# Gate product, inverse denominators and layer norm moved within a step of a scan-attention pipeline; routing and expert order and layout changed

## The chip, the cores and the metric

The kernel runs on one core of one Trainium2 chip. The metric is the time of one execution on the device in microseconds (us). Five engines work side by side, each through its own instructions in order: PE (TensorE; its weight loads are shown as PEld), DVE (VectorE), ACT (ScalarE), POOL (GpSimd) and SP (SyncE, which here only starts DMAs). They wait for each other on semaphores.

## The reference, cut to what matters

```python
# layer 0, x: (16, 128, 64, 64); 4096 positions a picture
u = gn(x) as tokens;  xs, z = split(u @ W_in)          # 2 x 256 channels
xc = silu(causal_conv4(xs) + conv_b)
dt, Bm, Cm = split(xc @ W_xproj)                       # 8, 16, 16
delta = softplus(dt @ W_dt + b_dt)
h = exp(delta * A) * h + delta * xc * Bm               # scan over positions, 16 states n
y = sum_n(h * Cm) + xc * D_param
x = x + (y * silu(z)) @ W_out
# layer 1, t: tokens of x
k, v = silu(ln(t) @ W_kv)                              # 8 heads
s = q . k;  m = cummax(s);  e = exp(s - m)
t = t + mean_over_heads(cumsum(e * v) / cumsum(e))
p = softmax over tokens of ln(t) @ gate_w.T            # 64 experts take their top 8 tokens
out_e = gelu(pooled_e @ weight1) @ weight2             # pooled: the 8 tokens weighted by p
t = t + scatter_add(out_e * p at the chosen tokens)
```

## The kernel before

**First stage: 137 steps.** A picture is 8 blocks of 512 positions, so there are 128 blocks. Step k (`for k in range(NK + LAG + 1)`, L712) scans block k. In the same step block k - 1 is finished (its y is turned, gated with z, multiplied by W_out), block k + 1 is prepared (convolution, projection, delta), and attention is done on block m = k - 9, whose second half is done one step later under the name `mp_`; layer norm of block m + 1 is done under the name `mn`. The last nine steps have attention only.

A step is a loop over the 16 states n (L898). In it, DVE multiplies bx = delta * xc * B (`product`, L355, 128 x 1024), then scans two halves of channels (`scan`, L361, 128 x 512 each); POOL multiplies h by C into the tile da (L375), and for odd n up to 7 starts a DMA that adds da of n - 1 onto da of n (`add_pair`). PE sums the 16 products over n by transposing matmuls into y_ps (`add_y`, `sums_of_y`, L892). ACT makes exp(delta * A) ahead of time: `decays(k, n, 2)` makes the next two tiles da. The rows B and C come broadcast from DRAM to bct (`load_bc`, by SP, three n ahead).

All engines are held to the order in which the program is written (`InOrder`, L23). So `beside(n)` (L736) is a list of what goes beside state n, written ahead of the scan, and `between(n)` (L724) is what DVE does between the two scans of n. A tile's buffers are handed out when the program is built. Matmul results go through three PSUM banks (`bank`, L224), which all the products of attention, convolution and projection share: a PE instruction that takes a bank waits for the instruction that last read it.

The functions of this change: `gate(k, a)` (L417, DVE) multiplies half a of the turned y, in PSUM as yb_ps, by z; it frees the bank of yb_ps. `conv` (L286) is the causal convolution as four matmuls per half into xs_ps, `conv_silu` (L295) its silu into xc on ACT, and `delta` (L324) two matmuls of 8 rows (dt_ps) and a softplus. `ln_center` (L456) makes cen_ps on PE, `ln_square` (L461) its square on ACT, `ln_var` (L466) var_ps on PE, `ln_scale` (L471) rstd on ACT (a Ln and an Exp), and `ln_apply` (L477) xn = cen * rstd on DVE at n = 14. `score_log`, `rest` and `split` (L553 to L578) cut two vectors in three bf16 parts each, `store_parts` (L580) writes them to DRAM, and `spread_parts` (L585) has SP read them back in 16 small DMAs into lh and rh. `weights` (L606) makes from lh and rh the exponents w_ps and on ACT the weights wm; `attend` (L623) multiplies them with v into ao_ps and sums the carry of a chunk, `carry_on` (L644) copies that carry on ACT, and `attend_before` (L648) adds the earlier chunks' part with e. `inverse` (L560) makes e, four Exps of 128 x 128. `gn_end` (L242) is group norm of the next picture, in parts that alternate between DVE, PE and ACT; it happens in the last but one step of a picture.

A table load on ACT (ACT_TABLE_LOAD) comes where the kind of function changes: into Exp/Ln (`load_exp`, L218) and back to Silu or Softplus.

**Second stage: routing** (L943 to L1134). 64 iterations, each over 512 tokens of two pictures, with work of 14 more behind them: PE turns the tokens (x_ps) and makes logits (l_ps); DVE takes mean and variance (`stats`), ACT makes rs, DVE nm and the scaled logits ls; PE turns ls into s_ps and ACT adds a bias into lg (`turn_logits`, L1028); ACT normalises the tokens in eight instructions into xn (`normed`, L1040). `choose` (L1055) takes the top 8 of each expert every eight iterations, `turn_chosen` and `pool_chosen` sum the chosen tokens, `turn_pooled` (L1101) turns the sums of a pair of pictures.

**Third stage: experts** (L1139 to L1180). 16 groups of four experts: SP loads w1 and w2, PE makes the hidden layer hps, ACT Gelu, PE turns it in four transposes, DVE copies, and PE multiplies by w2. **Fourth stage** (L1183): the experts' outputs are added to the tokens, unchanged here.

Of the kernel before, what the change touches and what calls it, by code (L numbers as in the profile page):

```python
# [8 lines left out]
F32 = mybir.dt.float32  # L9
# [6 lines left out]
P = 128  # L16
# [23 lines left out]
def conv_attn_hybrid(ctx: ExitStack, tc: tile.TileContext, x, w_in, conv_w, conv_b, w_xproj, w_dt, b_dt,  # L40
# [40 lines left out]
    with ExitStack() as st:  # L81
# [139 lines left out]
        def softplus(out_, in_, bias):  # L221
            ACT.activation(out_, in_, AF.Softplus, bias=bias)

        def bank(name):  # L224
            return ps.tile([P, L], F32, tag="ps", name=name)
# [98 lines left out]
        def delta(k):  # L324
            w = blocks[k]
            d = w["delta"] = mp.tile([P, NH2, L], F32, tag="delta", name="delta")
            for a in range(NH2):
                pt = bank("dt_ps")
                PE.matmul(pt, wdt[:, bass.ts(a, P)], w["dbl"][:R, :], start=True, stop=True)
                softplus(d[:, a, :], pt, bdt[:, a : a + 1])  # L330

        def delta_x(k):
            w = blocks[k]
# [378 lines left out]
        for k in range(NK + LAG + 1):  # L712
# [10 lines left out]

            def between(n):  # L724

                if m is not None:
                    if n == 4:
                        score_less(m)
                    if n == 6:
                        score_sum(m)  # L730
                if ends is not None and n == 5:
                    gn_end(ends, 2)
                if n == 15 and nxt is not None:
                    delta_x(nxt)

            def beside(n):  # L736
# [51 lines left out]
                    if ends is not None:  # L788
                        gn_end(ends, 1)
                if n == 5:  # L790
                    if prev is not None:
                        gate(prev, 1)
                    if mp_ is not None:
                        attend(mp_, 2)
                    if m is not None:
                        score_exp(m)
                    decays(k, n, 2)
                    if mp_ is not None:
                        carry_on(mp_, 2)
                        attend_before(mp_, 2)  # L800
                if n == 6:
                    if mp_ is not None:
                        weights(mp_, 3)
                    if prev is not None:
                        out_proj(prev)
                    if mp_ is not None:
                        attend(mp_, 3)
                    decays(k, n, 2)
                    if prev is not None:
                        put_back(prev)  # L810
                    if mp_ is not None:
                        carry_on(mp_, 3)
                    if ends is not None:
                        gn_end(ends, 3)
                if n == 7:
                    if m is not None:
                        score_log(m)
                        rest(m, 1)
                        split(m, 1)
                    if nxt is not None:  # L820
                        conv(nxt, 1, range(KC // 2))
                    decays(k, n, 2)
                    if m is not None:
                        rest(m, 2)
                        split(m, 2)
                        store_parts(m)
                        inverse(m)
                    if nxt is not None:
                        conv(nxt, 1, range(KC // 2, KC))
                        conv_silu(nxt)  # L830
                if n == 8:
                    if cur is not None:
                        sums_of_y(n)
                    if mp_ is not None:
                        attend_before(mp_, 3)
                        add_x(mp_, 1)
                        finish(mp_, 1)
                    if m is not None:
                        turn_weights(m)
                        value(m, 0, 0)  # L840
                    if nxt is not None:
                        xproj(nxt)
                        store_bc(nxt)
                    if m is not None:
                        value(m, 0, 1)
                    if ends is not None:
                        gn_end(ends, 4)
                if n == 9:
                    if mn is not None:
                        ln_center(mn)  # L850
                        ln_square(mn)
                    if cur is not None:
                        gate_silu(cur)
                    if k + 2 < NK:
                        load_block(k + 2, ACT)
                    if m is not None:
                        value(m, 1, 0), value(m, 1, 1)
                if n == 10:
                    if mn is not None:
                        ln_var(mn)  # L860
                    if nxt is not None:
                        delta(nxt)
                    load_exp()
                    if mn is not None:
                        ln_scale(mn)
                if n == 11:
                    if m is not None:
                        weights(m, 0)
                if n == 12:
                    if m is not None:  # L870
                        attend(m, 0)
                        attend_before(m, 0)
                    decays(k, n, 2)
                    if m is not None:
                        carry_on(m, 0)
# [22 lines left out]
            for n in range(N):  # L898
# [2 lines left out]
                if ends is not None and n == 2:  # L901
                    gn_end(ends, 0)
                beside(n)
                if n in (4, 11, 15):
                    decays(k, n, 2)
                if cur is not None:
                    later = k * N + n + LEAD_BC
# [5 lines left out]
                        add_pair(cur, n)  # L913
                else:
                    between(n)
                if cur is not None and n != 8:
                    sums_of_y(n)

                if 8 <= n <= 11 and i == 0 and prev is not None:
# [23 lines left out]
    with ExitStack() as st:  # L943
# [3 lines left out]
        AHEAD = 5  # L947
        xps = st.enter_context(tc.tile_pool(name="rxps", bufs=2, space=PSUM))
        lps = st.enter_context(tc.tile_pool(name="rlps", bufs=1, space=PSUM))
        sps = st.enter_context(tc.tile_pool(name="rsps", bufs=1, space=PSUM))  # L950
        acc = st.enter_context(tc.tile_pool(name="racc", bufs=1, space=PSUM))
        big = st.enter_context(tc.tile_pool(name="big", bufs=2))
        tsp = st.enter_context(tc.tile_pool(name="tsp", bufs=12))
# [145 lines left out]
                ACT.copy(ps, pl[:, :P])  # L1099

        def turn_pooled(p):  # L1101
            tp = acc.tile([P, L], F32, tag="plt", name="plt")
            PE.transpose(tp[:, :P], pair.pop(p)["ps"], ident)
            DVE.tensor_copy(pooled[:, :, 2 * p : 2 * p + 2], tp[:, :P].rearrange("p (j e) -> p e j", j=2))

        for it in range(AHEAD):
            load_tokens(it)
        for it in range(NIT + LATE + 2):
# [5 lines left out]
            if 0 <= it - 1 < NIT:  # L1114
                shifts(it - 1)
                scale_logits(it - 1)
                turn_logits(it - 1)
                normed(it - 1)
            if it < NIT:
                logits(it)  # L1120
                stats(it)
# [17 lines left out]
    with ExitStack() as st:  # L1139
# [11 lines left out]
        for e0 in range(0, E, EG):  # L1151
# [1 line left out]
            nc.sync.dma_start(w1, weight1[e0 : e0 + EG, :C, :].rearrange("e c h -> c e h"))  # L1153
            w2 = wpool.tile([P, EG, NHB, O], F32, tag="w2", name="w2")
            for e in range(EG):
                nc.sync.dma_start(w2[:, e], weight2[e0 + e, :HID, :].rearrange("(k p) o -> p k o", p=P))
            hps = ps.tile([P, HID], F32, tag="hps", name="hps")
            for e in range(EG):
                nc.tensor.matmul(hps[32 * e : 32 * e + 32, :], pooled[:, e0 + e, :], w1[:, e, :], start=True,
# [4 lines left out]
            nc.scalar.activation(hs, hps, AF.Gelu)  # L1164
            tps = ps.tile([P, NHB, P], F32, tag="tps", name="tps")
            for k in range(NHB):
                nc.tensor.transpose(tps[:, k, :], hs[:, bass.ts(k, P)], ident)
            ht = hp.tile([P, NHB, P], F32, tag="ht", name="ht")
            nc.vector.tensor_copy(ht, tps)
            ops = ps.tile([P, O], F32, tag="ops", name="ops")  # L1170
# [57 lines left out]
```

## Time and profile before

| what | us |
|---|---|
| median of 3 runs | 10505.95 |
| lowest, highest | 10497.34, 10506.3 |
| the profiled execution, its own time | 10500.43 |
| its span, first to last instruction | 10498.7 |
| first xn, last xn on DVE in the trace (first stage) | 617.2, 9587.7 |
| first and last nm on DVE (routing) | 9671.4, 10098.2 |
| first hps, last ht on PE and DVE (experts) | 10134.5, 10265.3 |
| first f_ps on PE (fourth stage) | 10280.5 |

The profile is of one execution. In its lines a group is an instruction as `out<-in` with its engine; nearly all of the first two stages have the line L31, that of the helper which records every operation, so tiles tell them apart. A timeline row gives the start, the duration, the instruction, how many were merged (x8), and in brackets how long its engine sat idle before it and what released it. A large matmul in fp32 stands as two rows (x2) of the trace. A table by windows gives the busy time of each engine in a stretch, then the clock that PE was granted (1.00 is full speed), the share of the DMA engines and GB/s.

### The profile page before, as it was taken

To read this page: it belongs to the slowest core of one execution; us is meant where nothing else is said; L and a number is where in the kernel's file an instruction comes from. 1 tells how busy PE (TensorE), PEld (TensorE's weight loads), DVE (VectorE), ACT (ScalarE), POOL (GpSimd) and SP (SyncE) were. 2 spreads that over 40 slices of the span, in tenths; PEclk is the share of its full clock that TensorE was granted. 3 is DMA by queue.
4 is the path that set the end of the run, shared out by engine and by line. 5 is a ranking of instruction groups with operands and counts; after the bars stand their busy time and mean duration, and the time that the engine had idled before them with its cause. 6 is when DMAs were issued, how large, how long until landed. Compare 5 with 4: busy or idle time off the path is not lost.

```text
span 10498.7 us, 163128 instructions
## 1 busy us (share of the span) xinstructions
PE 9306.2 (89%) x58461; PEld 5584.4 (53%) x58461; DVE 8947.7 (85%) x9987; ACT 7317.3 (70%) x12924; POOL 7411.9 (71%) x4387
## 2 busy tenths in 40 slices
PE   5689999999999999999999999999999999988775
PEld 3345555555555555555555555555555555545652
DVE  8999999999999999999999999999999999911743
ACT  5567777777777777777777777777777777755740
POOL 7887787878788777878787877788787878810000
PEclk7789999999999999999999999999999999998886
DMA  6676767676676667676766666676666667611358
GB/s 174 174 189 168 184 167 184 170 179 173 166 186 165 183 168 184 169 185 169 179 175 163 189 163 185 169 184 170 182 169 174 180 164 181 166 45 42 114 163 344
DMA packets 889083, 1794.65 MB, mean 171 GB/s; under 512 B 96896, under 2 KB 182544, under 8 KB 881104
## 3 DMA queue, kind: packets, MB, share of 16 engines
q1 hardware_dynamic: 732912, 1414.88, 48.0%
q0 software_dynamic: 73728, 268.47, 12.9%
q10 hardware_dynamic: 81632, 100.88, 3.0%
q8 instruction: 462, 7.57, 0.3%
q14 instruction: 349, 2.86, 0.1%
HBM read 1363.98 MB, written 151.52 MB: 144 GB/s over the span
## 4 chain that ended last, share of the span: by engine, by line
PE 46%; DVE 23%; ACT 18%; issue 9%; DMA 4%; ACTq 1%; SPq 0%; POOL 0%; DVEq 0%; POOLq 0%
DVE h L31 11%; DVE bx L31 8%; ACT da L31 7%; PE ao_ps L31 6%; PE y_ps L31 6%; PE v_ps L31 5%; PE xs_ps L31 4%; PE o_ps L31 4%; PE carry_ps L31 3%; PE k_ps L31 3%; PE dt_ps L31 2%; PE dbl_ps L31 2%; PE z_ps L31 2%; PE w_ps L31 2%; ACT wm L31 2%
## 5 line engine op out<-in xcount | busy, mean ns | idle before, releaser
L31 POOL TENSOR_TENSOR da<-h,bct 128x1024 f32<-128x1024 f32 x2048 | 6599.6, 3223 | 1718.2 <-DVE h L31 643.0
L31 DVE TENSOR_TENSOR_SCAN h<-da,state,bx 128x512 f32<-128x512 f32 x3584 | 4414.8, 1265 | 169.7 <-DVE bx L31 2.4
L31 DVE TENSOR_TENSOR bx<-du,bct 128x1024 f32<-128x1024 f32 x2048 | 2608.0, 1273 | 261.9 <-DMA bct<-bcs 195.0
L31 ACT ACTIVATE da<-delta,a_neg 128x512 f32<-128x512 f32 x4096 | 2603.0, 718 | 35.7 <-DMA da<-da 30.6
L31 PE MATMUL y_ps<-ident,da 128*128 128x128 f32 x12288 | 1773.8, 297 | 203.5 <-POOL da L31 103.8
L31 PEld LDWEIGHTS y_ps<-ident,da 128*128 128x128 f32 x12288 | 1534.0, 153 | 629.2 <-issue 372.6
L31 PE MATMUL v_ps<-wv,xn 128*128 128x512 f32 x2048 | 1031.5, 625 | 207.2 <-ACT xc L31 193.8
L31 PE MATMUL xs_ps<-xb,wc 128*128 128x512 f32 x2048 | 987.9, 620 | 141.3 <-DVE z L31 139.5
L31 PEld LDWEIGHTS ao_ps<-wm,v 128*128 128x128 f32 x8192 | 980.3, 193 | 244.2 <-issue 153.4
L31 ACT ACTIVATE v<-v_ps 128x512 f32<-128x512 f32 x1024 | 612.5, 600 | 681.6 <-PE v_ps L31 653.1
L31 PE MATMUL ao_ps<-wm,v 128*128 128x128 f32 x8192 | 1027.8, 279 | 54.7 <-ACT wm L31 45.3
L31 PE MATMUL k_ps<-xn,wk 128*128 128x512 f32 x2048 | 943.3, 594 | 0.0
L31 ACT ACTIVATE kt<-k_ps 128x512 f32<-128x512 f32 x1024 | 587.2, 600 | 207.6 <-PE k_ps L31 185.6
L31 PEld LDWEIGHTS v_ps<-wv,xn 128*128 128x128 f32 x2048 | 317.0, 188 | 758.6 <-ACT v L31 251.1
L31 ACT ACTIVATE wm<-w_ps 128x512 f32<-128x512 f32 x1024 | 555.9, 595 | 203.9 <-PE w_ps L31 197.8
L31 PEld LDWEIGHTS xs_ps<-xb,wc 128*128 128x128 f32 x2048 | 375.0, 198 | 567.4 <-issue 379.2
L31 DVE TENSOR_TENSOR_SCAN h<-da,bx 128x512 f32<-128x512 f32 x512 | 600.0, 1207 | 25.8 <-ACT w L31 0.5
L31 PEld LDWEIGHTS k_ps<-xn,wk 128*128 128x128 f32 x2048 | 370.3, 191 | 319.1 <-issue 253.1
L31 POOL COPY state<-h 128x2 f32<-128x2 f32 x1792 | 525.0, 293 | 0.0
L31 POOL DMA_DIRECT2D da<-da x512 | 449.9, 879 | 92.0 <-POOL state L31 52.6
L31 ACT ACT_TABLE_LOAD x395 | 506.8, 1283 | 9.9 <-issue 3.5
L31 ACT COPY carry<-carry_ps 128x128 f32<-128x128 f32 x512 | 133.6, 261 | 539.3 <-PE carry_ps L31 539.3
(196 smaller groups left out, 10678.1 us busy)
## 6 DMA issues: line engine op xcount, KB each, us to landing
bct<-bcs SPq DMA_DIRECT2D x2048, 512.0 KB
da<-da POOLq DMA_DIRECT2D x512, 512.0 KB, 7.8
xs<-t_d SPq DMA_DIRECT2D x240, 256.0 KB
xs<-in_x_dram SPq DMA_DIRECT2D x128, 256.0 KB
xt<-in_x_dram SPq DMA_DIRECT2D x64, 512.0 KB
t_d<-xt SPq DMA_DIRECT2D x64, 512.0 KB
t_d<-xs ACTq DMA_DIRECT2D x256, 128.0 KB
t<-t_d SPq DMA_DIRECT2D x128, 256.0 KB
```

Of the source, the lines that this page charges most:

```text
L31: return lambda *args, **kw: self.tc.keep_in_program_order(f(*args, **kw))
```

## The change

In the first stage: the second gate product goes from ahead of the scans of n = 5 to between the scans of n = 4. `gn_end` 2 goes from n = 5 to n = 6, part 3 from n = 6 to n = 7, part 4 from n = 8 to n = 10. `attend_before(mp_, 2)` goes behind `weights(mp_, 3)`, and the sums of y of n = 6 ahead of `out_proj`. `inverse` goes from n = 7 to n = 11, behind two decays. `ln_center` and `ln_square` go from the head of n = 9 to the end of n = 10, `ln_var` from n = 10 to the head of n = 12, `ln_scale` from n = 10 to n = 12 behind `attend`. `delta` issues both its matmuls ahead of both softplus. In routing, `normed` goes ahead of `turn_logits`, and the bank of s_ps is doubled, in exchange for the bank of `turn_pooled`, which now uses s_ps. In the experts' stage w2's 512 rows are spread over the partitions so that each partition reads four consecutive rows, and the transposes of hs read every fourth column to match.

```diff
         def delta(k):
             d = w["delta"] = mp.tile([P, NH2, L], F32, tag="delta", name="delta")
+            pt = [bank("dt_ps") for _ in range(NH2)]
             for a in range(NH2):
-                pt = bank("dt_ps")
-                PE.matmul(pt, wdt[:, bass.ts(a, P)], w["dbl"][:R, :], start=True, stop=True)
-                softplus(d[:, a, :], pt, bdt[:, a : a + 1])
+                PE.matmul(pt[a], wdt[:, bass.ts(a, P)], w["dbl"][:R, :], start=True, stop=True)
+            for a in range(NH2):
+                softplus(d[:, a, :], pt[a], bdt[:, a : a + 1])
...
             def between(n):
+                if n == 4 and prev is not None:
+                    gate(prev, 1)
                 if m is not None:
                     if n == 4:
                         score_less(m)
...
-                if ends is not None and n == 5:
+                if ends is not None and n == 6:
                     gn_end(ends, 2)
...
                 if n == 5:
-                    if prev is not None:
-                        gate(prev, 1)
                     if mp_ is not None:
                         attend(mp_, 2)
...
                         carry_on(mp_, 2)
-                        attend_before(mp_, 2)
                 if n == 6:
                     if mp_ is not None:
                         weights(mp_, 3)
+                        attend_before(mp_, 2)
+                    if cur is not None:
+                        sums_of_y(n)
                     if prev is not None:
                         out_proj(prev)
...
                         carry_on(mp_, 3)
-                    if ends is not None:
-                        gn_end(ends, 3)
                 if n == 7:
...
                         store_parts(m)
-                        inverse(m)
+                    if ends is not None:
+                        gn_end(ends, 3)
                     if nxt is not None:
                         conv(nxt, 1, range(KC // 2, KC))
                         conv_silu(nxt)
...
                         value(m, 0, 1)
-                    if ends is not None:
-                        gn_end(ends, 4)
                 if n == 9:
-                    if mn is not None:
-                        ln_center(mn)
-                        ln_square(mn)
                     if cur is not None:
                         gate_silu(cur)
...
                 if n == 10:
-                    if mn is not None:
-                        ln_var(mn)
                     if nxt is not None:
                         delta(nxt)
                     load_exp()
                     if mn is not None:
-                        ln_scale(mn)
+                        ln_center(mn)
+                        ln_square(mn)
+                    if ends is not None:
+                        gn_end(ends, 4)
                 if n == 11:
                     if m is not None:
                         weights(m, 0)
+                    decays(k, n, 2)
+                    if m is not None:
+                        inverse(m)
                 if n == 12:
+                    if mn is not None:
+                        ln_var(mn)
                     if m is not None:
                         attend(m, 0)
                         attend_before(m, 0)
+                    if mn is not None:
+                        ln_scale(mn)
                     decays(k, n, 2)
...
-                if n in (4, 11, 15):
+                if n in (4, 15):
                     decays(k, n, 2)
...
-                if cur is not None and n != 8:
+                if cur is not None and n not in (6, 8):
                     sums_of_y(n)
...
-        sps = st.enter_context(tc.tile_pool(name="rsps", bufs=1, space=PSUM))
+        sps = st.enter_context(tc.tile_pool(name="rsps", bufs=2, space=PSUM))
...
         def turn_pooled(p):
-            tp = acc.tile([P, L], F32, tag="plt", name="plt")
-            PE.transpose(tp[:, :P], pair.pop(p)["ps"], ident)
-            DVE.tensor_copy(pooled[:, :, 2 * p : 2 * p + 2], tp[:, :P].rearrange("p (j e) -> p e j", j=2))
+            tp = bank()
+            PE.transpose(tp[:, 0, :], pair.pop(p)["ps"], ident)
+            DVE.tensor_copy(pooled[:, :, 2 * p : 2 * p + 2], tp[:, 0, :].rearrange("p (j e) -> p e j", j=2))
...
                 scale_logits(it - 1)
+                normed(it - 1)
                 turn_logits(it - 1)
-                normed(it - 1)
...
-                nc.sync.dma_start(w2[:, e], weight2[e0 + e, :HID, :].rearrange("(k p) o -> p k o", p=P))
+                nc.sync.dma_start(w2[:, e], weight2[e0 + e, :HID, :].rearrange("(p k) o -> p k o", p=P))
...
-                nc.tensor.transpose(tps[:, k, :], hs[:, bass.ts(k, P)], ident)
+                nc.tensor.transpose(tps[:, k, :], hs[:, k::NHB], ident)
```

## The prediction, made before the changed kernel was run

> **What bounds the kernel now.** I read the page first, then the timelines of DVE, ACT and PE over one step of the first stage, then the waits of the routing stage.
>
> ```profile
> span 10498.7 us, 163128 instructions
> PE 9306.2 (89%) x58461; PEld 5584.4 (53%) x58461; DVE 8947.7 (85%) x9987; ACT 7317.3 (70%) x12924; POOL 7411.9 (71%) x4387
> ```
>
> No engine is full, so the bound is a ring of waits. The DVE timeline shows it at n = 13 and 14 of a step (columns: start, duration, then idle time before and its releaser):
>
> ```profile
> 5015.03 1.23 DVE L31 TENSOR_TENSOR bx<-du,bct 128x1024 f32<-128x1024 f32 x1
> 5016.40 2.45 DVE L31 TENSOR_TENSOR_SCAN h<-da,state,bx 128x512 f32<-128x512 f32 x2
> 5019.79 2.63 DVE L31 TENSOR_TENSOR bx<-du,bct 128x1024 f32<-128x1024 f32 x1 [0.94 <-DMA bct<-bcs]
> 5023.48 0.69 DVE L31 TENSOR_TENSOR xn<-cen_ps,rstd 128x512 f32<-128x512 f32 x1 [1.06 <-ACT rstd L31]
> ```
>
> A usual n takes 3.85 us with no idle time. DVE loses time at n = 14 alone: at the product bx (0.94 idle, and 1.40 more than its usual 1.23) and before xn, which waits for rstd. From one xn to the next, most steps take 71.5 us; over the 117 full steps (xn at 685.0 to 9143.4) the mean is 72.3. In 22 of these steps it is 73 to 74, and in 18 of them some matmuls of the convolution ran at half clock; in the other four, and in the ten steps above 74, DVE also waited for gs.
>
> rstd comes at the end of a PE and ACT chain that starts in the same step:
>
> ```profile
> 4981.83 0.37 PE L31 MATMUL w_ps<-rh,lh 64*128 64x512 bf16 x1 [0.37 <-ACT v L31]
> 4983.80 3.70 PE L31 MATMUL xs_ps<-xb,wc 128*128 128x512 f32 x8 [1.25 <-DVE z L31]
> 4992.96 1.98 PE L31 MATMUL o_ps<-z,wo 128*128 128x512 f32 x4 [0.74 <-ACT wm L31]
> 5007.74 1.12 PE L31 MATMUL v_ps<-wv,xn 128*128 128x512 f32 x2 [1.66 <-ACT xc L31]
> 5018.94 1.12 PE L31 MATMUL dt_ps<-dbl,wdt 8*128 8x512 f32 x2 [0.78 <-ACT delta L31]
> ```
>
> The convolution waits for the second gate product (DVE z) to free a PSUM bank. So the ring is: gate on DVE, 40 us of PE and ACT to rstd, xn on DVE, 26.1 us of unbroken DVE work (4951.94 to 4978.03) to the next gate 0. PE idles about 5 us in a step.
>
> **What the Trainium skill says.** "TensorE: Matmul & The Clock Gate", Part 1: PE runs at half rate after an idle window and at full rate after a busy one; the window free-runs at 3413 ns. The trace agrees. Its windows table (time, PE busy, PEld, DVE, ACT, POOL, granted clock, DMA) has, in the next step:
>
> ```profile
> 5126.21:5129.63 3.42, 1.68 (x8) 0.60 (x7) 3.38 (x4) 3.39 (x6) 2.53 (x1) 1.00 1.03 193
> 5129.63:5133.04 3.41, 3.41 (x5) 1.33 (x4) 3.24 (x4) 3.41 (x8) 2.25 (x2) 0.50 0.78 183
> ```
>
> 1.74 us idle, then a whole window at 0.50: the eight convolution matmuls took 5.40 us, not 3.70, and xn waited 2.77 us, not 1.06. I counted PE's idle time in every such window from 700 to 9500 us, taking the matmuls of 8 rows (dt_ps) as 7/8 idle: below 1.2 us none of 2,159 full-clock windows was followed by a halved one; from 1.8 us on 100 of 104 were. "ScalarE: Activation LUTs", What ACT_TABLE_LOAD costs: about 1283 ns, and a drain of 1380 ns. The trace has the 1283 (5020.80 to 5022.08); rstd starts at 5022.10, so no drain shows and I price 1.28. "DMA: Bandwidth & Descriptors", Specifications: 512 B is the least for line rate. Here 512 B packets of the experts' loads took 29.2 ns (17.6 B/ns) and those of 2 KB 96.4 ns (21.2), so there is still 17% to win.
>
> **The change, part by part.** I walk the chain of the step above; the ends of its ACT work are in this fence:
>
> ```profile
> 5004.42 1.28 ACT L31 ACTIVATE e<-x,off 128x128 f32<-128x128 f32 x4 [0.40 <-ACT parts L31]
> 5018.20 0.69 ACT L31 ACTIVATE delta<-dt_ps,bdt 128x512 f32<-128x512 f32 x1
> 5020.09 0.69 ACT L31 ACTIVATE delta<-dt_ps,bdt 128x512 f32<-128x512 f32 x1 [1.21 <-PE dt_ps L31]
> 5020.80 1.28 ACT L219 ACT_TABLE_LOAD   x1
> 5022.82 0.63 ACT L31 ACTIVATE rstd<-rstd 128x512 f32<-128x512 f32 x1
> ```
>
> (1) Gate 1 at n = 4, after the first scan: DVE ends it at about 4980.1 instead of 4983.74; DVE's work is the same. By the new instruction order the fourth v_ps takes its bank (0.2 late), and the convolution waits for ACT's v instead, done at 4981.9. It starts at 4982.1: 1.7 sooner. What now waits for DVE is v_ps, on gate 0 (4978.03).
> (2) y_ps of n = 6 moves ahead of o_ps: +0.87, minus the 0.74 that o_ps waited; weights(3) ahead of ao_ps must wait for ACT's carry copy, about +0.35. The place left behind carry_ps gains nothing, since rest_ps waits there for ACT. So parts are stored 1.7 - 0.5 = 1.2 sooner. SP's sixteen lh/rh loads and the bct load queued behind them move up by this, so bx at n = 14 ends at about 5021.2 and xn's operand is what is late next.
> (3) Inverse leaves n = 7: e (1.28) no longer stands between the parts and the table load; 1.3 of it is won at xc, which v_ps waits for. Total 2.5.
> (4) ln_center goes behind delta: -0.86 on PE ahead of the last v. It ends at 5016.79 - 3.4 = 5013.4.
> (5) Both dt_ps are issued first (ln_var, 1.05 on PE, is gone from before them): load 1.28 and two deltas of 0.69 without the 1.21. delta ends at 5016.1 instead of 5020.78.
> (6) But rstd is now behind more of ACT's queue: load 1.28, sq 0.60, two wm 1.1 with their wait, four da 2.45, four e 1.28, rstd 1.35. It ends at 5024.2 instead of 5023.45. Behind the DVE instruction that waits for it (xn) stand the scan of n = 14 and everything up to the next gate.
> So the ring is 0.7 longer: 71.5 + 0.7 = 72.2.
> (7) gn_end 2 to 4 move later, in 15 steps. Their DVE waits (2.91 at n = 5, 1.4 to 3.5 at n = 8) make ten of them 75 to 76 us. They vanish or fall into the wait for rstd, which is why I take 72.2 for all steps, against the mean of 72.3: 117 x -0.1 = -10.
> (8) What PE does with the time won: at w_ps(0) it is about 5 us ahead of before. It loses 0.9 at w_ps(1), whose bank now waits for xn (cen_ps is held longer), and 1.2 at the next ao_ps, because carry copy and wm stand behind rstd and da on ACT. It reaches the second v_ps about 3.5 us before gate 0 ends and waits there, in one piece. Of 3.5 us, more than 1.8 fall in one window for nearly every position of it, so the next window is halved: v_ps, w_ps and the convolution, all on the chain, lose between 0.8 and 1.7 us; I take 1.2. 117 x 1.2 = +140. The dt_ps pair without its gap is 1.5 us by my count, mostly under the threshold: I expect the halving of 5020.42 to go, which is off the chain before.
> (9) Routing. In a plain iteration (6.01 us) ACT's lg waits for rs, nm, ls, s_ps before the eight xn may start:
>
> ```profile
> ACT lg L31 <- PE s_ps L31: 117.2, 61, 4.4
> ```
>
> With xn first, ACT needs 0.2 + 2.74 + 0.6 + 0.5 + 0.6 = 4.65, PE (whose s_ps still waits for ls) some 5.0. Per eight iterations that is four plain ones at -1.0, one of 6.3 at -1.0, one of 9.7 at -1.0; the other two are full on DVE (4.41 us of not_equal; 2.33 and max). -6 for seven sets and -8 for the first eight: at most -50; I take -45 (-25 to -52). The second bank is part of it.
> (10) Experts: w2 in 2 KB packets: 32,623 x 29.2 ns / 16 engines = 59.5 us of transfer become 49.4. PE waited there 6.3 us for weights after the first group's 5.25 for w1. The transposes now read hs with a stride, not in the trace: 64 weight loads, from nothing to 0.1 us each. Value -4 (-10 to +6).
> The nine last steps, without scans, lose and gain the same parts of ACT's queue: nothing, +-10.
> Sum: -10 + 140 - 45 - 4 = +81. Against the profiled execution's own 10500.4 (span 10498.7 and 1.7 around it) that is 10581; the median of the runs is 5.5 above it, so 10587.
>
> **Rivals.** (A) No halving on the chain: faster. Place: the second v_ps. It decides if PE's wait there is under 1.8 us in a window, for which PE must lose 2 us more between w_ps(0) and gate 0. For: a halved window after the two waits of (8) would eat 1.7 of the lead, off the chain. Against: that needs a rare position of the window. Time: 10506 - 10 - 49 = 10447. (B) The dt_ps pair is halved as well, which now lies on the chain (w_ps(0) feeds wm ahead of rstd): 1.4 more per step, 10587 + 164 = 10751. For: 16 of 69 windows at 1.6 to 1.8 us were followed by a halved one. (C) The bct loads, not rstd, stay late: only if the parts are not stored sooner; then the ring is at least 72.3, and (8) stays: 10600, inside the forecast.
>
> **Numbers.** Forecast with (C) 0.50 (10530 to 10660); A 0.25; a halving worth only 0.3 to 0.6 us a step 0.12 (10485 to 10530); B 0.13. The range 10438 to 10685 leaves out about half of A's lower side and most of B. 0.2% (21 us) is about what a measurement of this kernel can tell from no change. Faster 0.27, same 0.11, slower 0.62.
>
> **What would show it.** xn to xn at 73 to 74 us; xn waiting 2 to 4 us for rstd; v_ps waiting 3 us for DVE z and a clock of 0.50 in the window after; no wait of xs_ps for z, of o_ps for wm, of the second dt_ps; routing's plain iterations at about 5 us. I am wrong if the steps fall below 72, if the wait before v_ps is short, or if rstd is no longer what xn waits for.

## The result and the profile after

The changed kernel takes 10665.95 us (median of 3, 10657.73 to 10676.55) against 10505.95: 1.0156 times the time before, 95% interval 1.0133 to 1.0179. It is slower, as forecast and inside the range, but by 160 us, not by 81. The sum of the prediction was made between profiled executions: there the forecast +81 stands against 10676.55 - 10500.4 = +176.

The head of its page:

```profile
span 10674.8 us, 163429 instructions
PE 9344.2 (88%) x58461; PEld 5604.6 (53%) x58461; DVE 8895.7 (83%) x9987; ACT 7276.2 (68%) x12924; POOL 7353.0 (69%) x4387
```

DVE is busy for 52 us less and the span is 176 longer, so its waits grew. A table of the stages, from the starts of xn, nm and hps in both traces:

| part (us) | before | after | change | forecast |
|---|---|---|---|---|
| start to first xn, and first step | 685.0 | 688.7 | +3.7 | 0 |
| 117 full steps | 8458.4 | 8650.0 | +191.6 | +130 |
| of these 103 usual ones, each | 71.93 | 73.56 | +1.63 | +1.5 |
| of these 14 with gn_end, each | 75.00 | 76.67 | +1.67 | -1.6 |
| nine last steps | 444.3 | 466.9 | +22.6 | 0 |
| routing, first to last nm | 426.8 | 388.7 | -38.1 | -45 |
| experts, first to last hps | 127.9 | 126.4 | -1.5 | -4 |

(The 117 steps are 72.29 us each before and 73.93 after; the forecast was 73.4 for every one, usual or not. The stretches between the stages change by -2 us in all. The fifteenth step with gn_end lies ahead of the first xn.)

DVE's timeline of the changed kernel at n = 14 of a usual step (start, duration, and in brackets idle time before and its releaser):

```profile
5417.09 1.27 DVE L31 TENSOR_TENSOR bx<-du,bct 128x1024 f32<-128x1024 f32 x1 [2.27 <-DMA bct<-bcs]
5421.94 0.69 DVE L31 TENSOR_TENSOR xn<-cen_ps,rstd 128x512 f32<-128x512 f32 x1 [3.57 <-ACT rstd L31]
```

Against the lines of before: xn waits 3.57 us, not 1.06, for rstd. ACT's timeline of the same place shows what stands ahead of rstd now:

```profile
5415.97 1.08 ACT L31 ACTIVATE wm<-w_ps 128x512 f32<-128x512 f32 x2 [0.28 <-PE w_ps L31]
5416.94 2.55 ACT L31 ACTIVATE da<-delta,a_neg 128x512 f32<-128x512 f32 x4
5419.40 1.27 ACT L31 ACTIVATE e<-x,off 128x128 f32<-128x128 f32 x4
5420.57 0.68 ACT L31 ACTIVATE rstd<-var_ps,eps 128x512 f32<-128x512 f32 x1
```

And PE's timeline 50 us earlier in that step:

```profile
5369.05 1.12 PE L31 MATMUL v_ps<-wv,xn 128*128 128x512 f32 x2
5373.89 5.49 PE L31 MATMUL v_ps<-wv,xn 128*128 128x512 f32 x6 [3.71 <-DVE z L31]
5379.31 0.61 PE L31 MATMUL w_ps<-rh,lh 64*128 64x512 bf16 x2
5380.19 3.70 PE L31 MATMUL xs_ps<-xb,wc 128*128 128x512 f32 x8
```

PE waits 3.71 us for gate 0, and the six matmuls behind it take 5.49 us, where at full clock they take 3.20 with their wait for gate 1 (the filler run below). The windows table (time, PE busy, PEld, DVE, ACT, POOL, granted clock, DMA) has the reason:

```profile
5369.68:5373.09 3.41, 0.49 (x2) 0.00 (x0) 3.38 (x3) 0.60 (x1) 3.02 (x3) 0.99 0.91 195
5373.09:5376.50 3.41, 2.62 (x3) 1.18 (x4) 3.34 (x10) 0.50 (x1) 3.24 (x3) 0.50 0.76 223
5376.50:5379.92 3.42, 3.42 (x10) 0.85 (x8) 3.22 (x5) 1.20 (x3) 1.62 (x2) 0.51 0.68 178
```

Not one window at half clock but two. The wait is longer than a window, so it reaches into the next; and that one, halved, has only 2.62 us of work in it. Of the 117 steps 55 have one halved window there (median 73.0 us) and 62 have two (74.0). They mostly alternate (107 of 116 times), which fits a step of 73.4 us being 21.5 windows of 3.413. The waits of the whole run that the two effects come from:

```profile
DVE xn L31 <- ACT rstd L31: 528.0, 127, 24.1
...
PE v_ps L31 <- DVE z L31: 452.3, 118, 4.3
...
DVE bx L31 <- DMA bct<-bcs: 270.3, 117, 5.1
```

The first was 296.9 before, the second 4.8 and the third 195.0. The waits of xs_ps for z (139.5 before), of o_ps for wm (87.1) and of dt_ps for delta (92.6) are gone, as the prediction said.

### The profile page after: what moved, and what is told of

Same layout as the page of the kernel before. It is cut to its first block, busy times and chain, and to the rows that moved or that the text cites. A ratio compares the mean times of both kernels' runs of the same rounds, so it can differ in the third digit from the quotient of the medians.

```text
span 10674.8 us, 163429 instructions
## 1 busy us (share of the span) xinstructions
PE 9344.2 (88%) x58461; PEld 5604.6 (53%) x58461; DVE 8895.7 (83%) x9987; ACT 7276.2 (68%) x12924; POOL 7353.0 (69%) x4387
## 5 line engine op out<-in xcount | busy, mean ns | idle before, releaser
L31 DVE TENSOR_TENSOR bx<-du,bct 128x1024 f32<-128x1024 f32 x2048 | 2567.2, 1254 | 336.8 <-DMA bct<-bcs 270.3
L31 PE MATMUL y_ps<-ident,da 128*128 128x128 f32 x12288 | 1631.3, 281 | 210.9 <-DMA da<-da 109.2
L31 PEld LDWEIGHTS y_ps<-ident,da 128*128 128x128 f32 x12288 | 1422.3, 145 | 575.9 <-issue 327.3
L31 PE MATMUL v_ps<-wv,xn 128*128 128x512 f32 x2048 | 1284.7, 752 | 497.2 <-DVE z L31 452.3
L31 PEld LDWEIGHTS ao_ps<-wm,v 128*128 128x128 f32 x8192 | 1004.2, 196 | 360.3 <-issue 219.8
L31 PEld LDWEIGHTS v_ps<-wv,xn 128*128 128x128 f32 x2048 | 430.7, 232 | 1138.3 <-DVE z L31 550.5
L31 PE MATMUL xs_ps<-xb,wc 128*128 128x512 f32 x2048 | 959.0, 604 | 3.8 <-issue 1.8
L31 DVE TENSOR_TENSOR xn<-cen_ps,rstd 128x512 f32<-128x512 f32 x128 | 88.6, 692 | 528.0 <-ACT rstd L31 528.0
```

The lines of the kernel that those rows point to most:

```text
L31: return lambda *args, **kw: self.tc.keep_in_program_order(f(*args, **kw))
```

## The experiments

My theory after the result: rstd, behind wm, decays and inverse on ACT, makes the ring longer, and through it PE runs ahead and waits at v_ps, where one or two halved windows per step add to the ring. The rival: the clock is beside the point, and the late rstd is the whole loss. All ratios are to the kernel before, run on the same chip, with their 95% intervals. A time "after xn" counts from the start of the last xn, and is a median over the 117 steps; gate 0 and gate 1 are the two gate products, on whose end v_ps waits; the long steps are the 14 with gn_end.

**Gate 1 alone, in the kernel before.**

```
 def between(n):
+    if n == 4 and prev is not None:
+        gate(prev, 1)
...
 if n == 5:
-    if prev is not None:
-        gate(prev, 1)
```

> The kernel before with one edit of the change alone: the second gate product goes between the two scans of n = 4. Theory (it is PE's early arrival, made by the other edits, that halves the clock): here PE reaches the second v_ps at 26.3 us after xn, as before, when gate 0 is done, so nothing is halved there; the convolution starts some 1.7 us sooner and so does everything behind it: 0.5 to 1.5 us less per step, 10,330 to 10,450. Rival (the moved gate itself makes PE run ahead and wait at v_ps): v_ps waits 2 us or more for DVE z, windows at v_ps are halved, and the time is 10,506 or more.

Measured: 10328.12 us, 0.9823 (0.9809 to 0.9838), 2 us below the expected range. The convolution starts at 30.02 us after xn (median) instead of 31.85, no window at v_ps is halved in any of the 117 steps, and usual steps take 70.43. The moved gate is a gain of some 180 us by itself; PE's early arrival is made by the other edits: the first v_ps ends at 25.9 us after xn here, at 22.2 in the changed kernel.

**The first v_ps four times, in the changed kernel.**

```
-value(mp_, x // 2, x % 2)
+value(mp_, x // 2, x % 2, 4 if x == 4 else 1)   # v_ps matmuls repeated so many times
```

> The changed kernel with the first v_ps of n = 3 computed four times instead of once: three more matmul pairs of 0.87 us each, into the same bank with the same result, fill the gap in which PE waits for gate 0. No wait is taken away and no work left out. Theory (the halved clock behind that gap lies on the ring, and costs one or two windows per step, 2.3 us from gate 0 to the convolution, not the 1.2 of the forecast): granted clock near 1 at v_ps, steps of 71.3 to 71.8 us, 117 x -2.0 to -2.3: 10,400 to 10,440. If a halving costs 1.2 as forecast: 10,525. Rival (the late rstd alone makes the step long, the clock is beside it): 10,640 to 10,690, or longer by the added matmuls.

Measured: 10668.35 us, 1.0152 (1.0137 to 1.0167): no change, as the rival had it. But the edit did two things. In the program's order of instructions the third v_ps now waits for gate 1 instead of for ACT: with a later first v_ps the banks are handed out in another order. So two v_ps come behind gate 1 (28.1 us), the convolution cannot start ahead of 30.9 even in the 63 steps with no halved window, and 1.13 us of wait for gate 0 and 1.05 for gate 1 still fall into one window in every other step. Inside the run, the 53 steps with one halved window there take 74.2 us (median) and the 63 without 72.7, which speaks for the clock; but the run as a whole settles nothing, and a filler that leaves the banks alone was needed (the fifth run).

**Layer norm's scale ahead of decays and inverse, in the changed kernel.**

```
 if n == 11:
     weights(m, 0)
+    ln_var(mn)
+    ln_scale(mn)
     decays(k, n, 2)
     inverse(m)
 if n == 12:
-    ln_var(mn)
     attend(m, 0)
     attend_before(m, 0)
-    ln_scale(mn)
```

> The changed kernel with ln_var and ln_scale moved ahead of the four decays and of the inverse denominators (n = 11 instead of n = 12); all else as changed. Theory (rstd ends last, and because xn is late against PE's own work, PE runs ahead of it and waits at v_ps): rstd ends 3.8 us sooner, xn waits under 1 us for it, bx at n = 14 for bct is what ends last, PE's wait at v_ps falls by 2 us or more and with it most halved windows: steps of 69 to 71 us, 10,180 to 10,380. Rival (the parts and bct hold the ring, rstd only fills their shadow): bx at n = 14 still starts at 69.3 after xn, steps of 71 us or more with the same halved windows: 10,330 to 10,420. If rstd's place does nothing: 10,666.

Measured: 10272.12 us, 0.9774 (0.9758 to 0.979). rstd ends at 69.1 us after xn instead of 73.9, PE's lead at v_ps is gone with it (the first v_ps ends at 25.4 instead of 22.2, gate 0 at 26.05), and 6 of 117 steps have a halved window there. 67 of the 103 usual steps take 70 to 71 us, and in these bx of n = 14 ends last. DVE's timeline there:

```profile
5407.23 3.15 DVE L31 TENSOR_TENSOR bx<-du,bct 128x1024 f32<-128x1024 f32 x1 [0.44 <-DMA bct<-bcs]
5410.29 0.68 DVE L31 TENSOR_TENSOR xn<-cen_ps,rstd 128x512 f32<-128x512 f32 x1
```

and POOL's:

```profile
5406.92 2.36 POOL L31 TENSOR_TENSOR da<-h,bct 128x1024 f32<-128x1024 f32 x1 [0.38 <-issue]
5409.23 1.19 POOL L31 COPY state<-h 128x2 f32<-128x2 f32 x1
```

The 1.23 us product takes 3.15, because it starts after POOL's product and has to let it end (at 5409.28); POOL's small copy then waits for DVE in turn (1.19 instead of 0.18). The Trainium skill says this in "SBUF — State Buffer", SBUF: two separate sides: a DVE operation with two SBUF inputs and a GpSimd operation that reads SBUF share a pair of ports, and whichever starts first holds it for its whole length. The trace agrees: 5409.28 + 1.23 is 0.13 us from the 5410.38 at which bx ends. It is also what the 2.63 us of bx in the prediction's first timeline were, which the prediction left unexplained. So a bct that lands between 67.2 and 69.4 us after xn, while POOL's product runs, gives much the same end, 70.6 to 70.7 in the median (in nine of ten such steps of this run between 69.7 and 71.0). In the steps under 70 us, 33 here, bx starts at 67.1 (median), ahead of POOL's product. The page makes no exception among DVE's operations with two SBUF inputs, but DVE's scans, which read da and bx from SBUF, do not show the lock: 1.26 us each beside POOL's product.

**Both of these edits together.**

```
+value(mp_, x // 2, x % 2, 4 if x == 4 else 1)
...
+    ln_var(mn)
+    ln_scale(mn)
     decays(k, n, 2)
```

> The two edits together: layer norm's scale ahead of the decays and the inverse, and the first v_ps of n = 3 four times. If the halving left in the run with the scale first is small, the added matmuls now lie on PE's way: equal to that run or up to 1 us per step longer (0 to +120 us). If PE still waits there with a halved clock, 1 to 2.3 us per step shorter than that run, 10,050 to 10,250.

Measured: 10381.49 us, 0.9877 (0.9862 to 0.9891): 109 us above the run with the scale alone. The convolution starts at 31.6 us instead of 30.0, by the same change of banks. It bears out only that there was no halving left to gain.

**A filler that leaves the banks alone, in the changed kernel.**

```
 for x in range(4, 8):
     value(mp_, x // 2, x % 2)
+    if x == 4 and cur is not None:
+        add_y(cur, -1), add_y(cur, -1), add_y(cur, -1)
```

> The changed kernel with the 8 transposes that start y_ps (n = -1) done three times more, between the first and the second v_ps of n = 3: they restart their banks, so nothing of the result changes, and they fill 2.6 us of the gap before gate 0. Unlike the run that repeated v_ps, the later v_ps take their banks in the order of the changed kernel (the third waits for ACT, the fourth for gate 1). Theory (one or two halved windows per step lie on the ring, 1.1 or 2.3 us, 1.7 in the mean): the convolution starts at 30.0 to 30.3 us after xn in all steps instead of 31.7, steps of 72.2: 117 x -1.7 = 10,466 (10,440 to 10,510). If halving costs the 1.2 of the forecast: 10,525. Rival (the late rstd alone; the clock does not matter): 10,640 to 10,690.

Measured: 10498.04 us, 0.999 (0.9981 to 0.9999), so 168 us off the changed kernel. PE's timeline:

```profile
5417.85 1.13 PE L31 MATMUL v_ps<-wv,xn 128*128 128x512 f32 x2
5418.81 3.34 PE L31 MATMUL y_ps<-ident,xc 128*128 128x128 f32 x24
5422.86 3.20 PE L31 MATMUL v_ps<-wv,xn 128*128 128x512 f32 x6 [0.72 <-DVE z L31]
...
5426.76 3.70 PE L31 MATMUL xs_ps<-xb,wc 128*128 128x512 f32 x8
```

The added calls of add_y do the eight transposes that start y_ps three times more: 24 needless transposes, 0.72 us of wait left, and the six matmuls take 3.20 us, not 4.54 or 5.49. No step has a halved window there; the convolution starts at 29.98; usual steps take 71.95 us, not 73.56. The halved clock is worth 1.61 us of each usual step, on the ring. The rival, by which the whole loss would stay, is out, and so is the thought that the clock is all of it: from here to the run with the scale first a usual step loses another 1.83 us (to 70.12). So a usual step is made up of 71.93 before, about -1.5 for the moved gate (70.43 in the first run), +1.5 for the late rstd and whatever else the other edits do (71.95), +1.6 for the clock (73.56).

**The group norm's ends early, in the changed kernel.**

```
-gn_end(ends, 1)    # n = 4, behind the convolution
-gn_end(ends, 2)    # n = 6, between the scans
-gn_end(ends, 3)    # n = 7
-gn_end(ends, 4)    # n = 10
+gn_end(ends, 1)    # n = 3, ahead of v_ps
+gn_end(ends, 2)    # n = 4, between the scans
+gn_end(ends, 3)    # n = 5
+gn_end(ends, 4)    # n = 6, between the scans
```

> The changed kernel with the group norm's ends early: part 1 at n = 3 (ahead of the v_ps), part 2 between the scans of n = 4, part 3 at the end of n = 5, part 4 between the scans of n = 6. Theory (in the 14 long steps ACT's copy for gs waits for PE behind the convolution, with decays and w behind it, and part 3's matmul waits for a bank in the middle of the second convolution; both lie ahead of the parts and of rstd): the waits of sum at n = 6 and of gs go, these steps fall from 76.7 to 73.6 to 74.3: 10,620 to 10,640. Rival (they only fill the shadow of rstd, as the prediction had it): within 10 us of the changed kernel.

Measured: 10629.05 us, 1.0113 (1.0098 to 1.0128), 37 us off the changed kernel; its 14 steps take 74.37 us instead of 76.67 (14 x 2.3 = 32 us). What the waits were, in DVE's timeline of the changed kernel:

```profile
5161.94 0.42 DVE L31 TENSOR_TENSOR_SCAN sum<-ones,w 128x128 f32<-128x128 f32 x1 [1.95 <-ACT w L31]
...
5179.94 0.21 DVE L31 TENSOR_SCALAR gs<-gs 128x1 f32<-128x1 f32 x1 [2.43 <-ACT gs L31]
```

The first wait is that of ACT's copy for gs, behind PE's convolution, with four da and w queued behind it; it lies ahead of the parts. ACT's timeline has it:

```profile
5159.09 0.16 ACT L31 COPY gs<-gn_ps 128x1 f32<-128x1 f32 x1 [1.51 <-PE gn_ps L31]
```

The second goes back to PE:

```profile
5178.99 0.38 PE L31 MATMUL gn_ps<-gs,gmat 128*128 128x1 f32 x2 [1.34 <-ACT parts L31]
```

a wait in the middle of the second convolution, with xc, v, delta and rstd behind it.

**Layer norm at its places of before, in the changed kernel.**

```
 if n == 9:
+    ln_center(mn)
+    ln_square(mn)
     gate_silu(cur)
 if n == 10:
+    ln_var(mn)
     delta(nxt)
     load_exp()
-    ln_center(mn)
-    ln_square(mn)
+    ln_scale(mn)
 if n == 12:
-    ln_var(mn)
...
-    ln_scale(mn)
```

> The changed kernel with layer norm's four operations at the places they had before (center and square at n = 9, var ahead of the two dt_ps, scale behind the delta); all else as changed, the inverse late too. Theory (layer norm behind PE's w_ps and behind wm, decays and inverse is the whole loss): rstd ends at 68 to 69 after xn, the bx of n = 14 sets the ring at 70.6 as in the two runs with 10,270 and 10,330, no halved windows at v_ps, and the nine last steps lose their 22 us: 10,240 to 10,270. Rival (the nine last steps are long for another cause): 10,270 to 10,290. If the late inverse or the dt_ps pair cost something by themselves: above 10,300.

Measured: 10305.78 us, 0.9807 (0.9793 to 0.9822): 360 us off the changed kernel, but 36 above the upper end of what the theory expected, and above 10,300, where I had put a cost of the late inverse or the dt_ps pair by themselves; neither was tried singly. The nine last steps are at 448.4 us (466.9 changed, 444.3 before), as expected. The rest of the miss is in the usual steps, 70.66 instead of 70.12: bct came in time for a step under 70 us in 6 of them, against 33 with the scale first. Why it comes later there I did not try. The nine last steps of the changed kernel, in PE's timeline:

```profile
9604.31 0.37 PE L31 MATMUL w_ps<-rh,lh 64*128 64x512 bf16 x1 [2.17 <-DMA rh<-pd]
...
9605.70 2.08 PE L31 MATMUL var_ps<-sq,mean_w 128*128 128x512 f32 x2 [0.68 <-ACT wm L31]
```

Layer norm's var now stands behind a w_ps that waits for the last of the rh loads, and rstd behind wm and e.

**Routing's and experts' edits alone, in the kernel before.** The first stage is left as it was.

```
-sps = st.enter_context(tc.tile_pool(name="rsps", bufs=1, space=PSUM))
+sps = st.enter_context(tc.tile_pool(name="rsps", bufs=2, space=PSUM))
...
     scale_logits(it - 1)
+    normed(it - 1)
     turn_logits(it - 1)
-    normed(it - 1)
...
-    nc.tensor.transpose(tps[:, k, :], hs[:, bass.ts(k, P)], ident)
+    nc.tensor.transpose(tps[:, k, :], hs[:, k::NHB], ident)
```

> The kernel before with the change's routing and experts' stages alone; the first stage as before. Routing's plain iterations at 4.8 instead of 6.0 us, -38 from first to last nm, experts -1 to -4, nothing else: 10,462 to 10,470 beside 10,506, so that the whole of the changed kernel's loss, some 200 us, is the first stage's. Rival (part of the routing gain needs the first stage's end as changed): less than -30.

Measured: 10471.66 us, 0.9968 (0.9957 to 0.998), -38 us; routing takes 388.5 us from first to last nm. The median is 2 us above the expected range.

**The bct load of n = 14 ahead of the lh and rh loads, with the scale first.**

```
-load_bc(*order[later])
+for at in ((later, later + 1) if n == 10 else () if n == 11 else (later,)):
+    load_bc(*order[at])
```

> The changed kernel with the scale ahead of decays and inverse, as in the run of 10,272, and on SP's queue the bct load for n = 14 ahead of the sixteen lh and rh loads instead of behind them. In the run of 10,272 bx of n = 14 ended at 70.66 after xn although it started at 67.65: it took 3.15 us instead of 1.23 while POOL's product of n = 13 ran. Theory (bct comes after POOL's product has begun, and the two exclude each other; so the ring stands at 70.6): with bct in time this bx starts ahead of POOL's product and takes 1.23, rstd at 69.1 sets the ring, steps of 69.1 to 69.4: 10,110 to 10,160. Rival (the long bx has another cause than bct's lateness, or the next bct becomes as late): 10,250 to 10,290.

Measured: 10673.51 us, 1.0148 (1.0123 to 1.0173): 401 us above the run with the scale alone, and far outside both expectations. One half of the theory held: bx of n = 14 starts at 67.1 without a wait, takes 1.23 us and ends at 68.4. DVE's and POOL's timelines at one n = 14:

```profile
5422.72 1.23 DVE L31 TENSOR_TENSOR bx<-du,bct 128x1024 f32<-128x1024 f32 x1
```

```profile
5422.82 3.33 POOL L31 TENSOR_TENSOR da<-h,bct 128x1024 f32<-128x1024 f32 x1 [0.38 <-PE y_ps L31]
```

But rstd ends at 73.3 (median), for a new wait, on ACT (engine, line waited for, us in total, times, longest):

```profile
ACT v L31 <- DMA bct<-bcs: 437.9, 102, 5.4
```

It was 50.6 us over 41 times with the scale alone. ACT stands at its issue of the bcs store (in one step from 5412.14, where dbl ends, to 5415.68) until a bct load has landed, and v, z and delta stand behind it:

```profile
5411.56 0.58 ACT L31 COPY dbl<-dbl_ps 40x512 f32<-40x512 f32 x1 [0.98 <-PE dbl_ps L31]
5415.68 0.33 ACTq L31 DMA_DIRECT2D bcs<-dbl  x1
5416.05 0.60 ACT L31 ACTIVATE v<-v_ps 128x512 f32<-128x512 f32 x1 [3.91 <-DMA bct<-bcs]
```

The transfers that SP and ACT start tell of their landing through eight semaphores, which the program hands out in turn, and the moved load shifted the turn. The traces have the number of each transfer's semaphore. In the step above the store has that of the bct load issued at 5410.77, whose last count comes at 5415.60. Over the run it shares its semaphore with a bct load in 102 of the 117 steps, and there it stands 399 us in all behind the end of dbl, against 3 us in the other 15. In the kernel before it shares with an lh load in all 117 steps and stands 27 us. With the scale alone it shares with a bct load in 89 steps, but stands only 0.9 us in each (median). Another order of the turns was not tried.

**The same, with the ends early and layer norm of the nine last steps as before.** The edits are those of the sixth run and, for `cur is None`, those of the seventh:

```
 if n == 9:
+    if cur is None:
+        ln_center(mn)
+        ln_square(mn)
...
+    if cur is None:
+        ln_var(mn)
     load_exp()
+    if cur is None:
+        ln_scale(mn)
```

> The same with two more edits: the group norm's ends early (as in the run of 10,629, where that took 37 us off), and in the nine last steps, which have no scans, layer norm at its places of before (as in the run with layer norm back, where that took 18 off). If the three gains add: 50 us under the run with the scale and bct alone, 10,060 to 10,110. If the ends' waits are already in the shadow of another wait there: 18 us under it.

Measured: 10670.76 us, 1.0151 (1.0134 to 1.0168), the same as without the two edits, and not the 18 us or more below it that were expected. The nine last steps gained 18 us (467.2 to 449.2), but the 117 steps lost 17: ACT's wait for bct is 491.9 us here. This run can't say whether the gains add; the last one can.

**The bct load alone, in the kernel before.**

```
-load_bc(*order[later])
+for at in ((later, later + 1) if n == 10 else () if n == 11 else (later,)):
+    load_bc(*order[at])
```

> The kernel before with that one SP edit alone: bct for n = 14 ahead of the lh and rh loads. Theory (before, rstd at 71.6 ends last and the late bct, with a bx of 2.6 us, lies in its shadow): bx of n = 14 takes 1.23 without a wait, xn waits for rstd that much longer, the time stays: 10,490 to 10,515. Rival (the bct loads set the ring of before, the third rival of the prediction): 10,400 or less.

Measured: 10567.99 us, 1.006 (1.0045 to 1.0076). bx of n = 14 takes 1.23 us with no wait, xn waits 642.4 us for rstd instead of 296.9, and usual steps take 72.20 instead of 71.93: the late bct was in rstd's shadow before, as expected. The loss, which I did not expect, is for the most part in the 14 long steps (78.83 instead of 75.00, 54 of 82 us), and ACT's v waits 76.9 us for bct loads, never so before: in one of these steps the issue of the bcs store stands from 5120.31 to 5123.85, as in the ninth run. In 27 steps the store shares its semaphore with a bct load, and stands 75 us in them.

**Three edits on the changed kernel: scale first, ends early, layer norm of the nine last steps as before.** They are those of the third and the sixth run, and for the last steps that of the tenth:

```
 if n == 3:
+    gn_end(ends, 1)
...
 if n == 11:
     weights(m, 0)
+    if cur is not None:
+        ln_var(mn)
+        ln_scale(mn)
     decays(k, n, 2)
```

> The changed kernel with three edits that each gained alone or in a larger set: layer norm's scale ahead of the decays and the inverse (10,272 by itself), the group norm's ends early (37 us off the changed kernel by itself), and layer norm at its places of before in the nine last steps (some 18 us); SP's order as changed. If the gains add: 10,272 - 14 x 2 - 18, that is 10,215 to 10,240, 2.6% under the kernel before. If the ends' waits hide behind the bx of n = 14 there: 10,250 to 10,260.

Measured: 10216.09 us, 0.9719 (0.9702 to 0.9735): 290 us under the kernel before and 450 under the changed one. It is in the range for gains that add. Steps with gn_end take 71.01 us, usual ones 70.08.

## Why the prediction was right in sign and wrong in size

Three terms of the sum failed: step (8), the halved clock, was sized at +140 and measured at +179; step (7) let the waits of gn_end "vanish or fall into the wait for rstd", and they cost 50 us more than that; the nine last steps were put at nothing and cost 23. The halved clock behind PE's wait at v_ps was foreseen, and it gives the change its sign: without it the kernel takes 10498, no more than before. So +81 became +176. Where a term is read without the halving, it is from the filler run (medians, after xn; before in brackets).

- (1) Right. The convolution starts 1.9 us sooner (29.98, was 31.85); forecast 1.7. Alone, this edit gains some 180 us.
- (2) Half right. Parts are stored 1.6 us sooner (50.5, was 52.1; forecast 1.2), but bx of n = 14 does not end sooner: 70.6, was 70.5; forecast 69.3. The step read "bx at n = 14 ends at about 5021.2". It took the longer bx to move with bct, while POOL's product fixes its end. It cost nothing here, since rstd ends later still; in the runs without the late rstd it is what the ring stands on.
- (3) to (5) Right: the last v ends 3.8 us sooner (forecast 3.4), delta 5.3 (forecast 4.7).
- (6) Right in direction, too large: rstd ends 0.2 later (71.8, was 71.6; forecast 0.7), and usual steps without halving take 71.95; forecast 72.2. Those 0.25 us are 26 us in the good direction, and that is luck: without them the result would have been some 10692, above the range's upper end of 10685.
- (7) Wrong. "They vanish or fall into the wait for rstd" does not hold: the waits moved to where they lie ahead of the parts and of the second convolution, so they lengthen the chain that rstd ends. Without halving these 14 steps take 75.75 us, not 72.2: 14 x 3.55 = +50 us. Moving them early took 37 us off.
- (8) Right place, too small. "I take 1.2", out of 0.8 to 1.7, was too low in that range: the halving costs 1.61 us in usual steps and (8650.0 - 8471.2) / 117 = 1.53 in the mean, +179 us instead of +140. I reckoned with one halved window. The wait, 452.3 / 118 = 3.8 us and not 3.5, is longer than a window, and in 62 steps a second one is halved: the convolution starts at 31.1 with one, 32.3 with two, 30.0 with none. That the dt_ps pair would not be halved was right (one halved window from 60 us after xn on in the 117 steps, 95 before), so rival B fell.
- (9) Routing -38 instead of -45. Plain iterations take 4.8 us (forecast about 5); among those with choose some are slower now (one of 8.3 takes 9.2).
- (10) Experts -1.5 instead of -4.
- The nine last steps, "nothing, +-10": wrong, +22.6. There the layer norm is behind w_ps, which waits for the rh loads; I counted ACT's queue and not PE's.

The misses: -26 (6), +50 (7), +39 (8), +23 (last steps), +7 and +2.5 (9, 10), +4 at the start, -2 between the stages, and -1 of rounding (117 x -0.1 was -11): +96, of 95. No single one makes the difference; step (7) and step (8) are the largest. Rival A, no halving on the chain, would have come out near the filler run, 10498, not at 10447, for the ends and the last steps are not in it. Rival C did not happen in the changed kernel: rstd ends after the bx of n = 14 in all 103 usual steps.

## What to carry to other kernels

An edit that makes an operation late on one engine makes another engine early elsewhere; if that is PE and it waits in one piece, its next matmuls pay in clock, and a wait longer than a window can pay twice (here in 62 of 117 steps). A wait that is moved does not vanish: look at its new place for what is queued behind it, on every engine that takes part. Try the edits of a bundle singly: here the moved gate product gained some 180 us, layer norm's scale behind decays and inverse cost about 390 with the halved clock that it brought, the late ends of the group norm cost 37 and layer norm's new place in the last steps 18. With these three put right the kernel is 2.8% faster than before. And when a load is moved, look at which transfer gets which completion semaphore: a load one place earlier cost 400 us.

## What the runs showed of the hardware

- In a window that is itself halved, far less idle time of PE keeps the clock halved. Of such windows in the 117 steps of the changed kernel none of the 123 with under 0.6 us idle was followed by a halved one, and all 62 with more were (before: none of 120, all 21). After windows at full clock the line is at about 1.8 us, as the prediction had it (below 1.6 us 5 of 2,141, from 1.8 us on 117 of 117), with the matmuls of 8 rows taken as 7/8 idle, as there.
- A DVE product with two SBUF inputs that starts 0.3 us after POOL's product takes 3.15 us (third run), and 1.23 us when it starts 0.1 us ahead of it (ninth run); POOL's product, which took 2.36 us in the first case, takes 3.33 in the second. Scans on DVE (1.26 us) run beside POOL's product unhindered.
- The issue of a transfer can stand until an earlier transfer of other data, which has the same completion semaphore, has landed: 3.5 us on ACT's queue in one step, 399 us in a run, after one load had been put one place earlier.
